# Sixteen blocks of edge rows, and ten tiles of nodes finished beside the last expert

## The chip, the cores and the metric

The kernel runs on one core of a Trainium2 chip. The metric is the device time of one execution in microseconds. The core has the engines PE (TensorE, matrix products), DVE (VectorE), ACT (ScalarE), POOL (GpSimd) and SP (SyncE, which here only issues DMAs). POOL issues DMAs too: all gathers and scatters, and some plain ones.

## The reference

A graph network of four layers over 3125 nodes with 256 features and 50000 edges. Each layer is a graph part and an expert part, both added to `x`. The change concerns the expert part of layer 0, and a little of what is checked before the layers begin:

```python
def _L0_ffn_ref(x, W_gat, att_src, att_dst, b_gat, ln_gamma, ln_beta, W1, b1, W2, b2, edge_index):
    ...
    h = (x_flat @ W_gat).reshape(M, HEADS, NUM_EXPERTS)          # 4 heads, 4 experts
    a_src = (h * att_src).sum(-1)
    a_dst = (h * att_dst).sum(-1)
    e = jax.nn.leaky_relu(a_src[src] + a_dst[dst], negative_slope=0.2)
    e_max = jax.ops.segment_max(e, dst, num_segments=M)
    ee = jnp.exp(e - e_max[dst])
    denom = jax.ops.segment_sum(ee, dst, num_segments=M)
    alpha = ee / (denom[dst] + 1e-16)
    msg = h[src] * alpha[:, :, None]
    agg = jax.ops.segment_sum(msg, dst, num_segments=M).reshape(M, HEADS * NUM_EXPERTS) + b_gat
    scores = _layernorm(agg, ln_gamma, ln_beta).reshape(M, HEADS, NUM_EXPERTS).mean(1)
    topk_s, topk_i = jax.lax.top_k(scores, TOP_K)                # the best 2 of 4
    w = jax.nn.softmax(topk_s, axis=-1)
    for ei in range(NUM_EXPERTS):
        g = jnp.where(topk_i == ei, w, 0.0).sum(-1)
        hh = jax.nn.gelu(x @ W1[ei] + b1[ei], approximate=False)
        out = out + g[..., None] * (hh @ W2[ei] + b2[ei])
```

`edge_index` of this part has 32768 edges, beside a loop at each node. After it the layer 1 graph part begins with a normalization of the new `x`, so it needs every expert's part of a node's row.

## The kernel before

**Layout.** Nodes lie in 25 tiles of 128 (`NT`, `P`), one node to a partition; `X` (25 x 256 floats a partition) stays in SBUF through all layers. `CHUNKS` are six groups of four tiles and one of a single tile: the seven chunks of columns that an expert works on.

**Order.** The framework puts the instructions of every engine into one order ahead of time, by dependencies, by the order in which they were written and by its own estimates of cost; each engine then runs its own order, and waits where a datum or a buffer isn't there. `with tc.issue_after(x)` makes the instructions written in it come behind `x` on `x`'s engine. A pool's tile name has as many buffers as the pool says (2 in `gx` and `wp`); a new tile of the name waits until the oldest is no longer read.

**Survey** (L63 to L208). Before the layers, faults in the indices are counted in the columns of `fault`, summed over the partitions by one matmul (L195) and the columns added (L197). `bad` chooses between the ordered arm (`body` with a plan), which is the one that runs here, and a general one. `gcnt` holds for each node the number of its edges; column 3 asks that none has more than `GK` = 40.

**The routed layer** (`routed_layer_in_order`, L1208). The edges have been ordered by destination before: `gsorted` holds the source of each, `gstart_i` the place where a node's edges begin. Then:

- `router_nodes` normalizes `X`, transposes it into `xt` and computes `hg`, `a_src` and `a_dst`. `node` (20 floats a node: `a_src` and `hg`) goes to DRAM as `nodes` (L1223).
- POOL gathers the row of each edge's source: 256 gathers of 128 rows (L1234, issued in the helper `gather`, L237). Edge `p*256+j` is in partition `p`, so the eight writes (L1236), each of 32 gathers, put a part of every partition's range into `edges`, and the table is only in order when all eight are done.
- The four experts run in `routed_experts` (L1194). A chunk is eight matmuls of 512 columns (L1204, `l0f_ph`), four gelus on ACT (L1205), sixteen matmuls of `project` (L580, `l0f_po`) and two evictions on DVE with the bias (L1292, called `put`). The values of expert 0 stay in SBUF (`y_first`), those of the others go to DRAM (`ytab`, L1294, on SP).
- `shares(d0, ...)` (L1250) takes five tiles of nodes. Five gathers fetch 40 consecutive rows of `edges` for each node (L1255), DVE adds `a_dst`, applies the leaky rectifier, masks what is past a node's count (`off`, L1261), subtracts the maximum; ACT takes the exp (L1265); DVE sums it (`den_`), multiplies the values by it (L1268) and adds them up in halves (L1273 to L1275, `num`). It is called behind chunks 2 to 6 of expert 3; its first DVE work stands behind the chunk's last eviction, its exp behind the chunk's last gelu.
- `router_gates` (L1118) makes the gates for all 25 tiles from `num` and `den_`: some forty small DVE instructions with a sqrt and an exp on ACT between them.
- The value steps (L1303 to L1314): `X += y * gate`, one DVE instruction per tile and expert, first for `y_first`, then with `l0f_yr` tiles of four tiles of nodes that SP loads from `ytab`.

Then `typed_values` (L1418) normalizes `X` again (`normalize`, L456: `bn_stats`, a reciprocal root for tiles 0 to 9, 10 to 19, 20 to 24, and one DVE instruction a tile), transposes it (L469) and begins the products of layer 1 (L1462).

Of the kernel before, what the change touches and what calls it, by code (L numbers as in the profile page):

```python
# [16 lines left out]
P = 128  # L17
# [24 lines left out]
GK = 40  # L42

# [19 lines left out]
def survey(ctx, tc, A):  # L63
# [9 lines left out]
    with ExitStack() as st:  # L73
# [70 lines left out]
        fault = sp.tile([P, 5], F32, name="sv_fault")  # L144
        V.memset(fault, 0.0)
        V.tensor_tensor(junk, nxt, ids["dst"], op=OP.is_lt)
# [47 lines left out]
        faults = ps.tile([1, 5], F32, name="sv_faults")  # L194
# [16 lines left out]
def body(ctx, tc, A, out, plan):  # L211
# [906 lines left out]
    def router_gates(ga, gate, sums, ones_):  # L1118

        den = ga.tile([P, NT, 4], F32, name="den")  # L1120
        V.tensor_scalar(den, ones_, 1e-16, None, op0=OP.add)
        V.reciprocal(den, den)
        ag = ga.tile([P, NT, 16], F32, name="ag", tag="hg")
        prod = ga.tile([P, NT, 16], F32, name="ag_sq", tag="prod")
        V.tensor_tensor(
            ag.rearrange("p t (h c) -> p t h c", h=4), sums, den[:, :, :, None].to_broadcast([P, NT, 4, 4]), op=OP.mult
        )
        bg = load(ga, bcast_rows(A["L0_ffn_b_gat"], 16), [P, 16], "bg")
        lg = load(ga, bcast_rows(A["L0_ffn_ln_gamma"], 16), [P, 16], "lg")
        lb = load(ga, bcast_rows(A["L0_ffn_ln_beta"], 16), [P, 16], "lb")  # L1130

        def all_tiles(x):
            return x[:, None, :].to_broadcast([P, NT, 16])

        V.tensor_tensor(ag, ag, all_tiles(bg), op=OP.add)
        mu = ga.tile([P, NT], F32, name="mu")
        V.tensor_reduce(mu, ag, axis=AX.X, op=OP.add)
        V.tensor_scalar(mu, mu, 1.0 / 16, None, op0=OP.mult)
        V.tensor_tensor(ag, ag, mu[:, :, None].to_broadcast([P, NT, 16]), op=OP.subtract)
        V.tensor_tensor(prod, ag, ag, op=OP.mult)  # L1140
        var = ga.tile([P, NT], F32, name="var")
        V.tensor_reduce(var, prod, axis=AX.X, op=OP.add)
        V.tensor_scalar(var, var, 1.0 / 16, None, op0=OP.mult)
        rs = ga.tile([P, NT], F32, name="rs")
        rsqrt(rs, var, EPS, ga, [P, NT])
        V.tensor_tensor(ag, ag, rs[:, :, None].to_broadcast([P, NT, 16]), op=OP.mult)
        V.tensor_tensor(ag, ag, all_tiles(lg), op=OP.mult)
        V.tensor_tensor(ag, ag, all_tiles(lb), op=OP.add)
        sc = ga.tile([P, NT, 4], F32, name="sc")
# [3 lines left out]
        rank = ga.tile([P, NT, 4], F32, name="rank")  # L1153
        beats = ga.tile([P, NT, 4], F32, name="beats")
        for j in range(4):
            to = beats if j else rank
            V.tensor_tensor(to[:, :, : j + 1], sc[:, :, j : j + 1].to_broadcast([P, NT, j + 1]), sc[:, :, : j + 1], op=OP.is_gt)
            if j < 3:
                V.tensor_tensor(to[:, :, j + 1 :], sc[:, :, j : j + 1].to_broadcast([P, NT, 3 - j]), sc[:, :, j + 1 :], op=OP.is_ge)
            if j:  # L1160
                V.tensor_tensor(rank, rank, beats, op=OP.add)
        best = ga.tile([P, NT], F32, name="best")
        V.tensor_reduce(best, sc, axis=AX.X, op=OP.max)
        V.tensor_tensor(sc, sc, best[:, :, None].to_broadcast([P, NT, 4]), op=OP.subtract)
        S.activation(sc, sc, AF.Exp)
# [3 lines left out]
        V.tensor_tensor(gate, gate, best[:, :, None].to_broadcast([P, NT, 4]), op=OP.mult)  # L1169
# [38 lines left out]
    def routed_layer_in_order():  # L1208

        with ExitStack() as st:  # L1210
# [5 lines left out]
            with ExitStack() as st2:  # L1216
# [7 lines left out]
                part = load(ga, gsorted[:, :].rearrange("(p j) o -> p (j o)", p=P), [P, GT], "src_parts", I32)  # L1224
# [4 lines left out]
                by_part = edges[:GE, :].rearrange("(p j) w -> p j w", p=P)  # L1229
                gx = pool(st2, "gat_e", 2)  # L1230
                for j0 in range(0, GT, 32):
                    ge = gx.tile([P, 32, 20], F32, name="ge")
                    for j in range(32):
                        gather(ge[:, j, :], nodes[:, :], part[:, j0 + j : j0 + j + 1])  # L1234

                    G.dma_start(by_part[:, j0 : j0 + 32, :], ge)  # L1236
# [4 lines left out]


                off = ga.tile([P, NT, GK + 1], F32, name="gat_off")
                V.tensor_tensor(
                    off, iota_f[:, None, : GK + 1].to_broadcast([P, NT, GK + 1]), plan["gcnt"][:, :, None].to_broadcast([P, NT, GK + 1]), op=OP.is_ge
                )
                V.tensor_scalar(off, off, NEG, None, op0=OP.mult)
                V.memset(off[:, :, GK:], 0.0)

                def shares(d0, dve, act):  # L1250

                    el = gx.tile([P, 5, GK + 1, 20], F32, name="el")
                    ds_ = slice(d0, d0 + 5)
                    for i in range(5):
                        gather(el[:, i, :GK, :].rearrange("p k w -> p (k w)"), edges[:, :], gstart_i[:, d0 + i : d0 + i + 1])  # L1255
                    with tc.issue_after(dve):
                        V.tensor_copy(el[:, :, GK, :], node[:, ds_, :])
                        s = gx.tile([P, 5, GK + 1, 4], F32, name="gat_s")
                        V.tensor_tensor(s, el[:, :, :, :4], a_dst[:, ds_, None, :].to_broadcast([P, 5, GK + 1, 4]), op=OP.add)
                        V.scalar_tensor_tensor(s, s, 0.2, s, op0=OP.mult, op1=OP.max)  # L1260
                        V.tensor_tensor(s, s, off[:, ds_, :, None].to_broadcast([P, 5, GK + 1, 4]), op=OP.add)  # L1261
                        V.tensor_reduce(top, s.rearrange("p d k h -> p d h k"), axis=AX.X, op=OP.max)
                        V.tensor_tensor(s, s, top[:, :, None, :].to_broadcast([P, 5, GK + 1, 4]), op=OP.subtract)
# [1005 lines left out]
```

## Time and profile before

| | us |
|---|---|
| three runs | 4818.13, 4819.55, 4824.78 |
| median | 4819.55 |
| the profiled execution | 4826.61 |
| its span in the profile | 4824.8 |
| busy in the span: PE, DVE, POOL, ACT | 4057.4, 2288.3, 1537.9, 1176.9 |
| the routed layer, from its first statistics (before 780) to layer 1's first transposed tile | to 1328.3 |
| the first matmul of the experts | 825.2 |
| the last matmul of the experts | 1222.1 |
| POOL: first gather of edge rows, last fetch of 40 rows | 835.0, 1234.8 |
| gates' last instruction | 1279.6 |
| value steps | 1279.9 to 1320.3 |
| PE's continuous run in layer 1 begins | 1348.4 |

The profile covers one execution. "Span" is the time from the first to the last instruction in it. In the lists, a line such as `L1234` is a line of the kernel; a line of a helper stands for all its callers, so the tile names tell them apart. "`a <- b`" is what an instruction writes and reads. Behind "idle before" stands what ended the idle time of the engine.

### The profile page before, as it was taken

What the parts mean: (1) busy time and instruction counts of PE and PEld (TensorE: products, weight loads), DVE (VectorE), ACT (ScalarE), POOL (GpSimd) and SP (SyncE); (2) the same over time, 40 slices, a digit from 0 to 9 for tenths busy, and PEclk for the clock granted to TensorE, in tenths of its full rate; (3) what the DMA queues carried; (4) which work ended last, traced back from release to release, by engine and by line L of the source; (5) the groups of instructions that cost most, each with busy time, mean ns of one, the idle gap of its engine ahead of it and who ended that gap; (6) DMA issues with size and microseconds to landing.
All of it is one profiled execution on the core that took longest, in us unless ns stands there. A gap on an engine that the chain in (4) does not pass through costs nothing. (4 is left out here: it accounts for less than half of the span.)

```text
span 4824.8 us, 54503 instructions
## 1 busy us (share of the span) xinstructions
PE 4057.4 (84%) x19973; PEld 2509.5 (52%) x20057; DVE 2288.3 (47%) x6392; ACT 1176.9 (24%) x2842; POOL 1537.9 (32%) x1497
## 2 busy tenths in 40 slices
PE   2488888996199996777699999899999997969989
PEld 2355544664066665555575555544444454634556
DVE  8987443112942237777668998610101033260053
ACT  0267721221122223444413222310202011210022
POOL 2067640775000007777505777300000002200010
PEclk6588889998599997887799999999999998989989
DMA  1046582122523347777524432022222322334200
GB/s 57 13 162 196 193 269 66 40 67 80 174 96 134 123 153 210 206 207 206 172 71 142 147 128 82 3 82 89 65 84 67 99 93 74 105 131 153 101 23 28
DMA packets 286835, 553.41 MB, mean 115 GB/s; under 512 B 81979, under 2 KB 195149, under 8 KB 275677
## 3 DMA queue, kind: packets, MB, share of 16 engines
q1 hardware_dynamic: 215804, 411.42, 25.4%
q0 software_dynamic: 70752, 138.40, 10.9%
q8 instruction: 160, 2.62, 0.2%
q14 instruction: 119, 0.97, 0.1%
HBM read 377.47 MB, written 172.20 MB: 114 GB/s over the span
## 5 line engine op out<-in xcount | busy, mean ns | idle before, releaser
L562 PE MATMUL agg_ps<-tt,h_l 128*128 128x512 bf16 (+3 forms) x3796 | 882.5, 394 | 56.8 <-ACT h_l L2049 46.3
L237 POOL DMA_INDIRECT h_kv<-kv_tab,kv_row x416 | 421.9, 1014 | 189.4 <-issue 68.2
L562 PEld LDWEIGHTS <-h_l 128*128 128x128 bf16 x3150 | 290.5, 98 | 331.7 <-issue 16.2
L240 POOL DMA_INDIRECT wgt_cells<-cw_wsum,cw_to x391 | 392.9, 1005 | 168.4 <-issue 112.2
L240 POOL DMA_INDIRECT gsorted<-gs_i,gpos x256 | 313.1, 1223 | 262.5 <-DVE gpos L913 176.7
L1646 PE MATMUL h_pq<-h_q,h_odt 128*128 128x256 bf16 x1248 | 219.6, 340 | 152.4 <-DVE h_qk L1648 152.3
L237 POOL DMA_INDIRECT ge<-nodes,src_parts x256 | 241.8, 945 | 232.9 <-PE l0f_po L580 155.2
L1846 DVE TENSOR_TENSOR at<-agg_ps,rdeg_r 128x512 f32<-128x512 f32 (+1 forms) x42 | 25.6, 633 | 586.5 <-PE agg_ps L562 586.5
L1966 POOL IOTA trash_slot<- 128x32 f32 x1 | 0.2, 158 | 863.4 <-PE l2g_ph L1865 863.4
L1791 ACT ACTIVATE l1f_h<-l1f_ph,bn_shift,bn_scale 128x512 f32<-128x512 f32 (+1 forms) x224 | 162.7, 731 | 384.9 <-PE l1f_ph L1788 384.9
L1646 PEld LDWEIGHTS <-h_odt 128*128 128x128 bf16 x1248 | 142.8, 118 | 209.7 <-issue 159.6
L562 PEld LDWEIGHTS agg_ps<-tt,h_l 128*128 128x128 f32 x700 | 126.3, 192 | 191.6 <-issue 190.9
L580 PE MATMUL l0f_po<-l0f_w,l0f_ht 128*128 128x256 f32 x800 | 180.6, 383 | 45.3 <-ACT l0f_ht L1205 45.3
L580 PE MATMUL l1f_po<-l1f_Wo,l1f_h 128*128 128x256 f32 x800 | 204.3, 388 | 2.3 <-DVE X L1797 1.4
L1697 PE MATMUL h_po<-h_kv,h_of 128*128 128x256 f32 x832 | 194.5, 394 | 8.1 <-DVE h_kv L1693 4.6
L1866 ACT ACTIVATE ht_next<-l2g_ph,l_bhid 128x512 f32<-128x512 f32 (+1 forms) x42 | 26.9, 641 | 714.4 <-PE l2g_ph L1865 714.4
L1788 PE MATMUL l1f_ph<-l1f_h,l1f_W 128*128 128x512 f32 (+1 forms) x448 | 195.4, 559 | 1.1 <-ACT l1f_h L1791 0.6
L580 PEld LDWEIGHTS l0f_po<-l0f_w,l0f_ht 128*128 128x128 f32 x800 | 153.4, 193 | 77.2 <-ACT l0f_ht L1205 46.1
L1788 PE MATMUL l1f_ph<-xt,l1f_W 128*128 128x512 f32 (+1 forms) x448 | 191.3, 547 | 0.9 <-PE l1f_pl L597 0.9
L580 PEld LDWEIGHTS l1f_po<-l1f_Wo,l1f_h 128*128 128x128 f32 x800 | 146.4, 190 | 84.0 <-issue 27.9
L469 PE MATMUL pt<-ident,xn 128*128 128x128 f32 x300 | 63.7, 369 | 149.6 <-DVE xn L458 109.9
L1204 PE MATMUL l0f_ph<-xt,l0f_w 128*128 128x512 f32 (+1 forms) x448 | 178.9, 549 | 3.0 <-ACT l0f_ht L1205 2.1
(628 smaller groups left out, 7482.7 us busy)
## 6 DMA issues: line engine op xcount, KB each, us to landing
tt<-cnt_ds SPq DMA_DIRECT2D x90, 640.0 KB
kv_tab<-kv SPq DMA_DIRECT2D x50, 1024.0 KB
tt<-wgt_cells SPq DMA_DIRECT2D x30, 1280.0 KB
wgt_cells<-cw_zero SPq DMA_DIRECT2D x6, 5800.0 KB
cw_row<-cell_r SPq DMA_DIRECT2D x23, 1128.0 KB
cw_ew<-in_ew_r_dram SPq DMA_DIRECT2D x22, 1108.0 KB
cnt_ds<-row_ds SPq DMA_DIRECT2D x150, 128.0 KB
cnt_sd<-cols SPq DMA_DIRECT2D x6, 3200.0 KB
```

Of the source, the lines that this page charges most:

```text
L237: return G.indirect_dma_start(out=dst, out_offset=None, in_=table, in_offset=bass.IndirectOffsetOnAxis(ap=idx, axis=0))
L240: G.indirect_dma_start(out=table, out_offset=bass.IndirectOffsetOnAxis(ap=idx, axis=0), in_=src, in_offset=None, **kw)
L469: T.transpose(pt[:, j, :], src[:, g + j, h * P : (h + 1) * P], ident)
L562: T.matmul(acc[h][:, :width], part[:, s, h * P : (h + 1) * P], tt[:, s - s0, :width], start=(s == 0 and i == 0), stop=(s == NT - 1 and i = ...
L580: T.matmul(psum, lhs[:, i, t * P : (t + 1) * P], rhs[:, i, :], start=(i == 0), stop=(bias is None and i == k - 1))
L1204: T.matmul(ph[:, :cl], w1[:, k, f * P : (f + 1) * P], xt[:, k, c : c + cl], start=(k == 0), stop=(k == 1))
L1646: T.matmul(pq[:, j, :], w["odt"][:, k0 + j, :], w["q3"][:, part, :], start=(part == 0), stop=(part == 2))
L1697: T.matmul(po, of[:, j, :], kv[:, j, D:], start=(k0 + j == 0), stop=(k0 + j == K - 1))
L1788: T.matmul(ph[:, :cl], ws[layer][:, k, o * P : (o + 1) * P], src[:, k, at : at + cl], start=(k == 0), stop=(k == 1))
L1791: S.activation(dst[:, o, :cl], ph[:, :cl], AF.Relu, bias=shi[:, col], scale=sca[:, col])
L1846: V.tensor_tensor(at[:, hf, c : c + cl], psum, rdeg_r[:, c : c + cl], op=OP.mult)
L1866: S.activation(nt_[:, o, c : c + cl], ph[:, :cl], AF.Relu, bias=b_hid[:, o : o + 1])
```

## The change

- `gsorted` is cut into sixteen blocks of 2048 consecutive edges instead of eight parts that run through all partitions, so the first blocks hold the edges of the first nodes. The tiles are divided into six parts, `GPARTS`: first tile, number of tiles, and the number of blocks that must be written before their fetches. Parts of 5 and 5 tiles need 6 and 11 blocks, 3 tiles need 14, and three of 4 tiles need all.
- The generator `rows_of_edges` writes the blocks that a part needs, gathers one block ahead, fetches the part's rows and yields. Two parts are asked for before the experts, and one more after each `shares`. Since a fetch of 40 rows can reach beyond what is written, the table is first filled with zeros (`blank`), and the survey counts as a fault any of the first three parts whose edges end later than its blocks allow.
- `off` now holds `a_dst` and the mask together, so one addition in `shares` goes.
- `shares` of part 0 stands behind chunk 1 of expert 2, part 1 behind chunk 2 of expert 3, the other four behind the last chunk. `gates` for tiles 0 to 9 stand at chunk 3 of expert 3, the exp in them behind its last gelu.
- All four experts' values go to `ytab`. For tiles 0 to 9 they are loaded on SP into `y_early` and added to `X` behind chunk 4 (experts 0 and 1) and chunk 5 (experts 2 and 3) of the last expert. The other fifteen tiles are loaded on POOL's queue after the gates.

The diff, shortened; `router_gates` has the same instructions on `n` instead of `NT` tiles, its three rows are loaded by `router_rows`, and its exp is put behind `ready` where that is given:

```diff
+GB = 16
+GPARTS = [(0, 5, 6), (5, 5, 11), (10, 3, 14), (13, 4, GB), (17, 4, GB), (21, 4, GB)]
+GEARLY = 10
...
-        fault = sp.tile([P, 5], F32, name="sv_fault")
+        fault = sp.tile([P, 8], F32, name="sv_fault")
         V.memset(fault, 0.0)
+        ready = sp.tile([1, 3], F32, name="sv_ready")
+        for i, (_, _, b) in enumerate(GPARTS[:3]):
+            V.memset(ready[:, i : i + 1], float(b * GE // GB - GK))
...
+        total_g = ps.tile([1, NT], F32, name="sv_total_g")
+        T.matmul(total_g, ones[:, :1], gcnt, start=True, stop=True)
+        upto_g = sp.tile([1, 3], F32, name="sv_upto_g")
+        for i, (d0, n, _) in enumerate(GPARTS[:3]):
+            V.tensor_reduce(upto_g[:, i : i + 1], total_g[:, : d0 + n], axis=AX.X, op=OP.add)
+        V.tensor_tensor(fault[:1, 5:8], upto_g, ready, op=OP.is_gt)
...
+                per = GT // GB
+                part = ga.tile([P, GB, per], I32, name="src_parts")
+                nc.sync.dma_start(part, gsorted[:, :].rearrange("(b p j) o -> p b (j o)", p=P, b=GB))
...
+                by_block = edges[:GE, :].rearrange("(b p j) w -> b p j w", p=P, b=GB)
                 gx = pool(st2, "gat_e", 2)
...
+                def rows_of(b):
+                    if b not in ge:
+                        ge[b] = gx.tile([P, per, 20], F32, name="ge")
+                        for j in range(per):
+                            gather(ge[b][:, j, :], nodes[:, :], part[:, b, j : j + 1])
+
+                def rows_of_edges():
+
+                    done = 0
+                    for d0, n, upto_block in GPARTS:
+                        for b in range(done, upto_block):
+                            rows_of(b)
+
+                            G.dma_start(by_block[b], ge[b])
+                        done = upto_block
+
+                        if done < GB:
+                            rows_of(done)
+                        el = gx.tile([P, 5, GK + 1, 20], F32, name="el")
+                        for d in range(n):
+                            gather(el[:, d, :GK, :].rearrange("p k w -> p (k w)"), edges[:, :], gstart_i[:, d0 + d : d0 + d + 1])
+                        fetched.append(el)
+                        yield
+
+                blank = gx.tile([P, 5, GK + 1, 20], F32, name="el").rearrange("p d k w -> p (d k w)")[:, :1280]
+                V.memset(blank, 0.0)
+                nc.sync.dma_start(edges[:GE, :].rearrange("(p a b) w -> p a (b w)", p=P, a=4), blank[:, None, :].to_broadcast([P, 4, 1280]))
...
+                off = ga.tile([P, NT, GK + 1, 4], F32, name="gat_off")
+                V.tensor_scalar(past, past, NEG, None, op0=OP.mult)
+                V.tensor_tensor(
+                    off, past[:, :, :, None].to_broadcast([P, NT, GK + 1, 4]), a_dst[:, :, None, :].to_broadcast([P, NT, GK + 1, 4]), op=OP.add
+                )
+
+                rows = rows_of_edges()
+                next(rows)
+                next(rows)
...
-                        V.tensor_tensor(s, el[:, :, :, :4], a_dst[:, ds_, None, :].to_broadcast([P, 5, GK + 1, 4]), op=OP.add)
+                        V.tensor_tensor(s, el[:, :, :, :4], off[:, ds_], op=OP.add)
                         V.scalar_tensor_tensor(s, s, 0.2, s, op0=OP.mult, op1=OP.max)
-                        V.tensor_tensor(s, s, off[:, ds_, :, None].to_broadcast([P, 5, GK + 1, 4]), op=OP.add)
...
+                def take(y, e, t0, end, dve=None):
+
+                    n = min(4, end - t0)
+                    (nc.sync if dve is not None else G).dma_start(y[:, :n], ytab[e][:, t0 : t0 + n, :])
+                    for t in range(t0, t0 + n):
+                        with tc.issue_after(dve) if dve is not None else ExitStack():
+                            V.scalar_tensor_tensor(X[:, t, :], y[:, t - t0, :], gate[:, t, e : e + 1], X[:, t, :], op0=OP.mult, op1=OP.add)
...
-                    ys = y_first[:, t0 : t0 + n, :] if e == 0 else wp.tile([P, 4, D], F32, name="l0f_ys")[:, :n]
+                    ys = wp.tile([P, 4, D], F32, name="l0f_ys")[:, :n]
...
-                    if e:
-                        nc.sync.dma_start(ytab[e][:, t0 : t0 + n, :], ys)
-
-                    k = c // 512 - 2
-                    if e == 3 and k >= 0:
-                        shares(5 * k, put.ins, last.ins)
...
+                    nc.sync.dma_start(ytab[e][:, t0 : t0 + n, :], ys)
+
+                    for i, at in enumerate([(2, 1), (3, 2), (3, 6), (3, 6), (3, 6), (3, 6)]):
+                        if at == (e, c // 512):
+                            shares(i, put.ins, last.ins)
+                            next(rows, None)
+                    if (e, c // 512) == (3, 3):
+                        gates(0, GEARLY, last.ins)
+                    if e == 3 and c // 512 in (4, 5):
+                        for t0 in range(0, GEARLY, 4):
+                            for i in range(2):
+                                take(y_early[:, GEARLY * i :][:, t0:GEARLY], 2 * (c // 512 - 4) + i, t0, GEARLY, put.ins)
+
+                y_early = stage[0].tile([P, NT, D], F32, name="l0f_y_early", tag="xn")
                 routed_experts(wp, ps, b1, xt, keep)
-                router_gates(ga, gate, num.rearrange("p t (h c) -> p t h c", h=4), den_)
+                gates(GEARLY, NT)
             with ExitStack() as st2:
                 yp = pool(st2, "l0f_yp", 3)
...
+                for t0 in range(GEARLY, NT, 4):
+                    for e in range(4):
+                        take(yp.tile([P, 4, D], F32, name=f"l0f_yr{e}"), e, t0, NT)
```

## The prediction

> **What bounds the kernel now.** I read the page first, then the waits and busy times between 780 and 1420 us, then the timelines of the engines there.
>
> ```profile
> span 4824.8 us, 54503 instructions
> ...
> PE   2488888996199996777699999899999997969989
> DVE  8987443112942237777668998610101033260053
> ...
> POOL 2067640775000007777505777300000002200010
> ```
>
> A slice is 120.6 us. PE is full nearly everywhere, with a hole in the eleventh slice (1206 to 1327 us), where DVE shows 9 and then 4: the end of the routed layer.
>
> ```profile
> 825.00:1137.00 312.00, 311.21 (x1110) 207.46 (x1110) 33.35 (x53) 66.64 (x101) 229.47 (x246) 1.00 0.22 50
> 1137.00:1183.00 46.00, 0.73 (x2) 0.50 (x2) 8.17 (x7) 2.86 (x3) 26.51 (x29) 0.53 0.33 100
> 1183.00:1222.00 39.00, 37.25 (x138) 26.22 (x136) 35.81 (x33) 13.66 (x18) 10.73 (x10) 0.94 0.40 132
> 1222.00:1328.00 106.00, 0.13 (x1) 0.00 (x0) 98.10 (x221) 7.63 (x9) 4.73 (x5) 0.52 0.52 174
> ```
>
> Columns: stretch, length, busy PE, PEld, DVE, ACT, POOL, granted clock, DMA share, GB/s. The experts run at full rate to 1137, stand for 46 us, end at 1222, and then PE waits 106 us for DVE. The waits say who ends each hole:
>
> ```profile
> PE pt L469 <- DVE xn L458: 107.1, 2, 106.2
> ...
> DVE gat_s L1259 <- DMA el<-edges,gstart_i: 45.9, 1, 45.9
> ACT gat_s L1265 <- DVE gat_s L1263: 65.5, 4, 45.5
> ...
> PE l0f_po L580 <- ACT l0f_ht L1205: 45.3, 1, 45.3
> ```
>
> The first hole is a queue: the first shares' exp stands in ACT's order before a gelu, the exp waits for DVE, and DVE for edge rows that POOL fetches.
>
> ```profile
> 1160.64 0.58 POOL L1236 DMA_DIRECT2D edges<-ge  x1 [1.99 <-DMA ge<-nodes,src_parts]
> 1163.39 0.97 POOL L237 DMA_INDIRECT el<-edges,gstart_i  x1 [2.17 <-DMA edges<-ge]
> ...
> 1261.36 0.33 SPq L1415 DMA_DIRECT2D ty_r<-in_type_r_dram  x1
> ...
> 1279.93 29.29 SPq L1311 DMA_DIRECT2D l0f_yr<-l0f_y  x21
> ```
>
> POOL starts at 835.0 and has all 256 gathers and eight writes out only at 1160.64. Later, loads of expert values start at 1279.93, when the gates are done.
>
> From 1350 to 1700 us every 50 us hold 50.00 us of PE work at clock 1.00, so what PE gains before 1350 is kept behind it, one for one. My mark is 1348.4, where PE becomes continuous (L1462).
>
> **The change part by part.** *Survey.* One matmul, three reduces, one compare. Rows of the same size: L195 0.19 us, L197 0.15 us, with gaps 0.2 to 0.3, so 0.2 + 0.3 + 4 x 0.17 = 1.2 us. The body's first instructions start at 66.1, where a DMA issued at 62.50 has just landed, while the fault flag is done at 63.12; that may hide all. Bounds 0 and +1.5; I take +1.2.
>
> *Start of the layer.* The index load now comes in 64-byte runs; it is issued at 785.7 and used at 835.0, so 49 us cover it. A memset of 1280 elements (L1442, 1024 in 0.91: 1.1 us) and a write of 2.6 MB of zeros are added. At the 289 GB/s of 1262 to 1280 the write takes 9 us. SP has nothing between 803.4 and 827.5, and the first block is written only at 855. Should it meet the node table (issued 827.5), POOL starts up to 9 us later: 0 to +9, I take 0. The 4100-element add that makes the offsets (L1268: 3280 in 3.56, so 4.45 us) fits before DVE's first eviction at 836.5 (8.57 us idle). In return 1.03 us (L1261) leaves each shares call.
>
> *POOL's order.* Gathers follow each other every 1.249 us, and a write adds 0.6 (878.75 to 880.60 holds one gather and one write). First rows: 112 gathers and 6 writes, then five fetches. They start at 835.0 + 112 x 1.249 + 6 x 0.6 = 978.5. Five fetches took from 1163.39 to 1173.74, 10.4 us, to land, so they are there at 989. The shares that use them stand behind the eviction of expert 2, chunk 1: 1026.7 + 0.7. Second: 197 gathers before, 11 writes, so start 1087.7 and landing at 1098, against an eviction at 1126.9. So both exps find their data, with 38 and 29 us to spare, and the 45.3 us stall goes. A write after fetches must wait until they have landed, because they read the same table: with two block buffers at most one further block (20 us) can be put ahead of a fetch, which stays inside that room.
> Fourth part: 269 gathers, 16 writes, then the last block must land and be written and land: 2.0 + 2.2 as at 1158 to 1163. 835.0 + 336.0 + 9.6 + 4.2 = 1184.8. The three waits for fetches to land cost 0 (other gathers fill them) to 4.4 each (1169.3 to 1173.7); I take 3 in all: 1188. Landing of four fetches, 9 us: 1197 (bounds 1194 and 1207).
>
> *The last expert.* An expert takes 86.5 us (last evictions 912.64 and 999.13), so without stalls the last eviction is at 1172.1. Added to ACT: two exps with sqrt and exp of the early gates, each with table loads of 1.28 on both sides. In 1183 to 1222 three such breaks cost PE 39.0 - 37.25 = 1.75 us; at worst each costs 1.28 + 0.89 + 1.28 = 3.45. Four breaks: 2 to 14 us, I take 5, so PE ends at about 1177.
> The Trainium skill, page "ScalarE: Activation LUTs", section "What ACT_TABLE_LOAD costs", has 2.66 us for every switch, of which 1.38 is a drain. The row disagrees: the load at 1204.36 lasts 1.28 and its gelu starts at 1205.65. By the rule the four breaks would be at most 4 x 6.2 = 25 us, by the row at most 14.
> DVE from 1127 on: shares 14.5 (the sum of the rows of L1257 to L1275 without L1261), gates 10 (before 18.7, less four memsets of 0.91, a wait of 2.6 and 2.5 for the smaller tiles), forty value steps at 0.40 = 16, seven evictions 4.4: 45 us in the 50 until 1177. It just fits; the early loads, twelve more on SP, where only seven stores an expert stand, have 14 us between chunks. In 1183 to 1222 DVE was 92% busy and PE still ran at 95%.
>
> *Shares of the last fifteen tiles.* Three tiles: 9.5 us, from 1177, done by 1190, before the fourth part's rows land. Then three times four tiles, 12 each (14.5 x 0.8 = 11.6 if proportional, 14.5 at most): 1197 + 36 + 1 for an exp = 1234. The fetches of parts five and six need buffers that come free at 1190 and 1209, and land 9 us after, before their turn.
>
> *Gates and values.* Before, 1261.2 to 1279.9, 18.7 us, of which four memsets are 3.6 and a wait for `pri` 2.6. The later layer's loads that hold `pri` back start when the shares' buffers are free, as at 1261.36. With fifteen tiles instead of 25: 12 to 18.7, I take 16. The first value step then needs loads: expert 0's values no longer lie in SBUF, which covered that time with 9.98 us of L1306. A POOL write took 2.75 from issue to landing (1160.64 to 1163.39): +3. First step at 1253. Sixty steps at 28.98/73 = 0.397: 23.8, to 1277.
> The sixteen loads move from SP to POOL. Before, 9.4 MB came in 29.29 us; now 7.5 MB need 23.4 us at that rate, as much as DVE needs.
> The Trainium skill, "SBUF — State Buffer", section "Who interferes with whom", speaks against this: a DVE instruction with two SBUF inputs blocks a GpSimd instruction that reads SBUF. By it each of the sixteen issues could wait a whole step, 16 x 0.48 = 8 us if nothing hid it. Beside a busy DVE 25 fetches took 0.997 on average instead of 0.945, 16 x 0.05 = 1 us, so I add nothing.
>
> *Behind the values.* From the last step (1320.3) to PE's continuous run (1348.4) are 28.1 us of DVE statistics and normalization. Ten tiles are now finished early. Their statistics (10 x 0.56) and normalization (3.3) may fill DVE's waits. Bounds 0 and -13 (with a share of the transposes' copies); I take -6.
>
> **The sum.** 1277 + 28.1 - 6 = 1299 against 1348.4: -49.4; with the survey +1.2: -48. The profiled execution took 4826.6 us (1.8 outside its span), 7.1 over the median of the three runs shown, 4819.55; the difference is set against that median: 4772 us. The likeliest case's own range is 4752 to 4790.
>
> **Rivals.** *Early values slip.* DVE has 45 us of work in a room of 50. If gates and value steps of the ten tiles end up behind the last expert, 26 us return to DVE's tail: 4772 + 26 = 4798. For it: DVE takes instructions in order, and a wait for sqrt or a load holds all behind it. Against: the 92% above.
> *The order itself is the new wait.* Shares of part four placed ahead of part three's second half leave DVE standing until 1197 with 8 us undone, and a late POOL start adds 9: 4789. For it: at 1191.84 the next group's L1259 ran between an earlier group's L1273s.
> *POOL's queue bounds the tail (slower).* If loads issued on POOL land one after another at L1236's rate, 320 KB in 2.75, then 7.5 MB take 66 us instead of 23.8, +42. The next layer's loads (5.6 MB on SP, 19 us) share the same stretch: 4772 + 42 + 19 = 4833. It decides above 4.5 us a load ((23.8 + 48)/16). For it: no row shows large loads on that queue. Against: 2.75 is mostly time to land, and gathers issued every 1.25 overlap.
> *The change does not do what it says*: the first exp still waits. That needs rows 38 us later than reckoned; the stall would be back and only the ten tiles' move would remain, about 4819 - 15 = 4804.
>
> **How the numbers follow.** Forecast 0.60; early values slip 0.13; the order 0.09; no early exp 0.04; POOL's queue 0.08; what I have not seen 0.06, half of it slower. About 0.2%, 9.6 us, is what a measurement can tell from no change. Forecast, slip and order are faster, and most of the fourth: 0.83 with a little of the rest; same 0.06; slower 0.11. The range 4745 to 4805 takes in the bounds above (landing 1194 to 1207, breaks 2 to 14, normalization 0 to -13) and the two mild rivals.
>
> **What would show it.** Right: no PE wait above 10 us between 825 and 1170; the last eviction between 1172 and 1186; the fourth part's rows landed by 1207; sixty value steps within 30 us; PE continuous near 1300. Wrong: an exp that waits over 10 us for DVE in the experts; forty value steps behind the last expert; gaps between the last sixty steps that end on a DMA.

## The result, and the profile after

The changed kernel takes 4805.85 us (median of 8 runs, 4803.55 to 4810.51), the kernel before 4823.22 us beside it (8 runs, 4818.13 to 4824.78): ratio 0.9967, 95% interval 0.9958 to 0.9976. That is 17 us faster, where 48 were forecast, and 0.85 us above the upper end of the range. The profiled execution has a span of 4801.7 us against 4824.8.

From the page of the changed kernel: span, and busy tenths in 40 slices (120.0 us each).

```profile
span 4801.7 us, 54722 instructions
...
PE   2488888997099987677699999899999997969978
...
DVE  8987443124732337777669998600101033260053
...
POOL 2067640777100017777406777300000002200010
```

PE's hole is still in the eleventh slice (1200 to 1320 us), now with a 0 in it. The same stretches as before, with the same columns (stretch, length, busy PE, PEld, DVE, ACT, POOL, granted clock, DMA share, GB/s):

```profile
1137.00:1183.00 46.00, 38.05 (x148) 26.33 (x147) 36.37 (x93) 15.06 (x22) 37.47 (x30) 0.96 0.35 104
1183.00:1222.00 39.00, 0.00 (x0) 0.00 (x0) 8.14 (x14) 1.29 (x2) 16.12 (x18) 0.50 0.28 85
1222.00:1328.00 106.00, 13.77 (x63) 10.03 (x64) 95.16 (x239) 12.02 (x18) 16.14 (x24) 0.52 0.48 159
```

The first hole is gone: the experts run on and end at 1175.6 us. But from 1183 to 1222 us DVE, which has to do the rest, works 8.14 of 39 us. The waits between 780 and 1420 us (engine, tile, line, what it waited for: us in total, times, longest) and POOL's timeline (start, us, operation, idle time before and its end) name the reason.

```profile
POOL l0f_yr L1339 <- DVE gate L1189: 37.1, 1, 37.1
DVE gat_s L1314 <- DMA el<-edges,gstart_i: 32.9, 2, 20.4
...
POOL el L250 <- DVE el L1312: 23.5, 1, 23.5
```

```profile
1037.31 3.91 POOL L250 DMA_INDIRECT ge<-nodes,src_parts  x1 [0.30 <-issue]
...
1138.57 3.27 POOL L250 DMA_INDIRECT ge<-nodes,src_parts  x1 [0.30 <-issue]
...
1161.53 5.24 POOL L250 DMA_INDIRECT ge<-nodes,src_parts  x1 [0.30 <-issue]
...
1177.55 3.66 POOL L250 DMA_INDIRECT ge<-nodes,src_parts  x1 [0.30 <-issue]
...
1193.99 0.94 POOL L250 DMA_INDIRECT el<-edges,gstart_i  x1 [0.30 <-issue]
...
1201.85 1.15 POOL L1270 DMA_DIRECT2D edges<-ge  x2 [4.42 <-DMA el<-edges,gstart_i]
1205.39 1.00 POOL L250 DMA_INDIRECT el<-edges,gstart_i  x1 [2.39 <-DMA edges<-ge]
...
1233.74 0.95 POOL L250 DMA_INDIRECT el<-edges,gstart_i  x1 [23.54 <-DVE el L1312]
```

Four single gathers took 3.9, 3.3, 5.2 and 3.7 us; eight more take 1.1 to 1.6, the others 0.94. Then come the third part's fetches (1193.99), behind all of block 15's gathers; then both remaining writes, which waited 4.42 us until those fetches had landed; then the fourth part's fetches (1205.39); and the fifth part's only at 1233.74, after 23.54 us of waiting for a buffer. DVE's timeline shows what it did with the rows:

```profile
1201.34 0.67 DVE L1314 TENSOR_TENSOR gat_s<-el,gat_off 128x492 f32<-128x492 f32 x1 [20.39 <-DMA el<-edges,gstart_i]
1214.53 0.84 DVE L1314 TENSOR_TENSOR gat_s<-el,gat_off 128x656 f32<-128x656 f32 x1 [12.52 <-DMA el<-edges,gstart_i]
...
1232.89 0.58 DVE L1329 TENSOR_REDUCE gat_num<-el 128x48 f32<-128x240 f32 x1
```

The first line is the third part (3 tiles, 492 = 3 x 41 x 4), the second the fourth. In DVE's order the fourth part's add stands directly behind the third's, so the third part, whose rows were there at 1201, is summed only at 1232.89. The shares end at 1269.8, the gates at 1280.0, the value steps run from 1284.93 to 1309.1, and PE's first typed product follows at 1319.65. The first product with `lin_v` starts at 1333.44, before at 1353.59: 20.15 us earlier.

### The profile page after: what moved, and what is told of

It is laid out like the page before. It is cut to its first block, busy times and chain, and to the rows that moved or that the text cites. A ratio compares the mean times of both kernels' runs of the same rounds, so it can differ in the third digit from the quotient of the medians.

```text
span 4801.7 us, 54722 instructions
## 1 busy us (share of the span) xinstructions
PE 4045.5 (84%) x20059; PEld 2493.3 (52%) x20059; DVE 2295.5 (48%) x6445; ACT 1182.8 (25%) x2849; POOL 1568.8 (33%) x1521
## 5 line engine op out<-in xcount | busy, mean ns | idle before, releaser
L1712 PE MATMUL h_pq<-h_q,h_odt 128*128 128x256 bf16 x1248 | 205.9, 324 | 161.8 <-DVE h_qk L1714 161.6
L250 POOL DMA_INDIRECT ge<-nodes,src_parts x256 | 257.2, 1005 | 232.9 <-PE l0f_po L593 155.2
L1763 PEld LDWEIGHTS h_po<-h_kv,h_of 128*128 128x128 f32 x832 | 160.4, 195 | 31.7 <-DVE h_kv L1759 5.4
L1714 DVE TENSOR_TENSOR h_qk<-h_kv,h_pq 128x512 f32<-128x512 f32 (+1 forms) x220 | 141.6, 650 | 60.9 <-DMA h_kv<-kv_tab,kv_row 48.5
## 6 DMA issues: line engine op xcount, KB each, us to landing
tt<-wgt_cells SPq DMA_DIRECT2D x30, 1280.0 KB
```

The source lines that it names most:

```text
L250: return G.indirect_dma_start(out=dst, out_offset=None, in_=table, in_offset=bass.IndirectOffsetOnAxis(ap=idx, axis=0))
L1712: T.matmul(pq[:, j, :], w["odt"][:, k0 + j, :], w["q3"][:, part, :], start=(part == 0), stop=(part == 2))
L1714: V.tensor_tensor(qk[:, :n], kv[:, :n, :D], pq[:, :n], op=OP.mult)
L1763: T.matmul(po, of[:, j, :], kv[:, j, D:], start=(k0 + j == 0), stop=(k0 + j == K - 1))
```

## Experiments

All edits are against the changed kernel, and L numbers are its lines. Ratios are to the kernel before, run beside each set. "Shares' end" is the end of the last L1329 in the profile (in `no_edges`, whose lines are shifted, L1332). Each profile is one execution. Where the kernel before takes 4822 us, the first gather of edge rows starts between 833.9 and 836.9 us, at 836.85 in the changed kernel's profile: up to 3 us between two profiles can be this start and not the edit.

**The first set** asked which of three things in series held the tail: POOL's order, DVE's order, the buffers. Its kernels ran where the kernel before takes 5699 us, with PE and ACT standing up to 100 us at a time beside POOL's gathers, so that the experts end at 1648 to 1662 us, long after POOL: its ratios say little of the 17 us and are not to be held against 0.9967.

`pool_order`: a block's gathers wait, on POOL, for the last fetch ahead of them.

```diff
-                        for j in range(per):
-                            gather(ge[b][:, j, :], nodes[:, :], part[:, b, j : j + 1])
+                        with tc.issue_after(fetch[-1]) if fetch else ExitStack():
+                            [gather(ge[b][:, j, :], nodes[:, :], part[:, b, j : j + 1]) for j in range(per)]
...
+                            at = gather(el[:, d, :GK, :].rearrange("p k w -> p (k w)"), edges[:, :], gstart_i[:, d0 + d : d0 + d + 1])
+                        fetched.append(el), fetch.append(at.ins)
```

> POOL's order alone is put right: the gathers of a block wait, on POOL, for the last fetch that stands ahead of them in the program, so the three fetches of the third part go ahead of the last twelve gathers of block 15. My theory is that three things in series cost the tail: POOL's order, DVE's order and the two fetch buffers. By it the third part's rows land at 1179 instead of 1201 us, but DVE still has the fourth part's add ahead of the rest of the third part, so that gives nothing by itself; the writes no longer wait 4.4 us for the fetches: the fourth part lands at 1211 instead of 1214.5 and the stage ends 3 to 4 us earlier (time -0.1%). The rival, that POOL's order alone is what was lost, has the shares' end 15 to 20 us earlier (-0.4%).

`dve_order`: from the fourth part on, a part's first two steps stand behind the last reduce of the part before.

```diff
-                    with tc.issue_after(dve):
+                    with tc.issue_after(summed[-1] if i > 2 else dve):
...
-                    V.tensor_reduce(num[:, ds_, :], el[:, :, :5, 4:].rearrange("p d k w -> p d w k"), axis=AX.X, op=OP.add)
+                    summed.append(V.tensor_reduce(num[:, ds_, :], el[:, :, :5, 4:].rearrange("p d k w -> p d w k"), axis=AX.X, op=OP.add).ins)
```

> DVE's order alone: the copy and the add that begin the shares of parts four, five and six stand behind the last reduce of the part before. My theory: the third part is then done at 1210 us, in time in which DVE stood idle; its buffer comes free 23 us earlier, so the fifth part's rows are there when the fourth is done (1226.5), and the shares end at 1250 instead of 1269.8: time -20 us (-0.4%). The rival, that POOL's order alone is what was lost, has under 5 us here. A second rival, stretched gathers, has nothing here.

`both_orders` has both edits.

> Both orders. My theory: third part done by 1195 us, fourth from 1211 to 1223, the shares end at 1245 to 1247 instead of 1269.8, time -23 us (-0.5%), so the two are not a sum of equals: DVE's order is most of it. The rival (POOL's order alone) has here what it has without DVE's order, -15 to -20.

`third_buffer`: the fifth part's rows go into the tile of the early values (tag `xn`).

```diff
-                        el = gx.tile([P, 5, GK + 1, 20], F32, name="el")
+                        el = gx.tile([P, 5, GK + 1, 20], F32, name="el") if d0 != 17 else stage[0].tile([P, NT, D], F32, name="el_x", tag="xn").rearrange("p t d -> p (t d)")[:, :4100].rearrange("p (d k w) -> p d k w", d=5, k=GK + 1)
```

> A third buffer for fetched rows: the fifth part's rows go into the tile that held the early values, so that their fetches need not wait for the fourth part. My theory, buffers as the smallest of the three terms: POOL's idle 23.5 us before the fifth part's fetches goes, its shares start 8 us earlier, the sixth part's fetches still wait for a buffer; shares' end 6 us earlier (-0.12%). If the buffers were the main cause: shares' end 15 us or more earlier.

Measured: 0.9957 (0.9941 to 0.9973), 0.9998 (0.9979 to 1.0017), 0.9956 (0.9939 to 0.9973), 0.9971 (0.9953 to 0.9988). The ratios alone would speak for the rival that POOL's order was what was lost, but the traces don't: the copy L1312 of the third part, which stands behind the last expert, starts at 1653.0, 1667.2, 1656.3 and 1664.7 us, and the differences between the ratios follow it in the main. The two kernels with POOL's order have their experts done some 10 us earlier; why was not tried. What can be read is the tail behind that copy, to the shares' end: 56.1, 55.2, 55.3 and 46.6 us. With the third and fourth parts' rows landed long before, DVE's order is worth 1 us and the buffer 9, both against `pool_order`; the changed kernel itself is not in this set.

**Orders, one more time, with two new questions.** The two orders were run again, where the kernel before takes 4822 us; all sets from here on ran so.

> DVE's order alone, once more: in the first set every kernel, the one before too, took 18% longer than in its own profile (5699 us against 4823), with PE, ACT and DVE standing still for up to 100 us at a time while POOL gathered, so the experts ended long after POOL and the orders hardly met. Where the kernel before takes 4823 us, my theory has the third part done at 1210 us, the shares' end at 1250 instead of 1269.8 and a ratio to the kernel before of 0.9925 (the changed kernel has 0.9967). The rival, POOL's order alone: 0.996 to 0.997. Where the kernel before takes 5700 us again: 0.998 to 1.000, as in the first set.

Measured: 0.9934 (0.9920 to 0.9947). DVE's timeline:

```profile
1200.07 0.67 DVE L1314 TENSOR_TENSOR gat_s<-el,gat_off 128x492 f32<-128x492 f32 x1 [21.46 <-DMA el<-edges,gstart_i]
...
1211.94 0.59 DVE L1329 TENSOR_REDUCE gat_num<-el 128x48 f32<-128x240 f32 x1
...
1213.75 0.84 DVE L1314 TENSOR_TENSOR gat_s<-el,gat_off 128x656 f32<-128x656 f32 x1 [0.98 <-DVE rs_r L448]
...
1255.25 0.73 DVE L1329 TENSOR_REDUCE gat_num<-el 128x64 f32<-128x320 f32 x1
```

The adds of the third and the fourth part start about 1 us earlier than before the edit (1200.07, 1213.75), but the third part is now summed at 1211.94 instead of 1232.89, in time that DVE had stood idle. The shares end at 1256.0, 13.8 us earlier (14 of the 20 expected), and PE's first typed product comes at 1305.76, 13.9 earlier. Of the 13.8, 0.8 are the rows and 13 the edit: from the fourth part's add to the shares' end are 42.2 us where the changed kernel has 55.3.

> Both orders once more. Where the kernel before takes 4823 us: my theory has the fourth part from 1211 to 1223, the shares' end at 1245 to 1247 and a ratio of 0.992; the rival (POOL's order is what was lost, DVE's nothing) has the same with and without DVE's order and a ratio of 0.993 to 0.994. Where it takes 5700 us: 0.9956, as in the first set.

Measured: 0.9940 (0.9926 to 0.9954), shares' end 1256.5. The third part's fetches go out at 1169.70 and it is summed at 1192, 20 us earlier than with DVE's order alone, and nothing comes of it: the fourth part's fetches still start at 1204.97. POOL has the same gathers to make before them in whichever order. So DVE's order is the loss, and POOL's adds nothing to it that can be seen: counted from the first gather (835.45 here, 833.93 in `dve_order_2`) the shares end 1 us earlier. POOL's order alone was run only in the first set.

`one_input`: the forty early value steps read X alone; the experts' values of ten tiles are left out.

```diff
-                            V.scalar_tensor_tensor(X[:, t, :], y[:, t - t0, :], gate[:, t, e : e + 1], X[:, t, :], op0=OP.mult, op1=OP.add)
+                            if dve is not None:
+                                V.tensor_scalar(X[:, t, :], X[:, t, :], gate[:, t, e : e + 1], 0.0, op0=OP.mult, op1=OP.add)
+                            else:
+                                V.scalar_tensor_tensor(X[:, t, :], y[:, t - t0, :], gate[:, t, e : e + 1], X[:, t, :], op0=OP.mult, op1=OP.add)
```

> The forty early value steps read X alone (X times gate plus zero) and leave the experts' values of ten tiles out; their loads and their place stay. It asks what stretched single gathers to 3.3, 5.2 and 3.7 us. If DVE instructions with two inputs from SBUF keep POOL from its descriptors: the gathers beside the early steps go back to 0.94 us, only the one beside the shares' product (3.3 us) stays, and the rows of blocks 14 and 15 are there some 9 us earlier; the time falls by 5 to 9 us from the changed kernel's 0.9967 to 0.995 to 0.996. If DMA traffic or a busy DVE of any kind stretched them: the same long gathers, and a time within 2 us of the changed kernel's.

Measured: 0.9942 (0.9929 to 0.9956), shares' end 1260.2, 9.6 us earlier; 2.1 of them are the earlier start of this execution (first gather at 834.72). The early steps and the first fetch of the third part, from the timelines of DVE and POOL:

```profile
1156.32 6.11 DVE L1343 TENSOR_SCALAR X<-X,gate 128x256 f32<-128x256 f32 x20
...
1170.76 6.39 DVE L1343 TENSOR_SCALAR X<-X,gate 128x256 f32<-128x256 f32 x20
```

```profile
1184.58 0.95 POOL L250 DMA_INDIRECT el<-edges,gstart_i  x1 [0.30 <-issue]
```

DVE is busy in two runs of over 6 us, and no gather beside them takes over 1.1 us; the fetches start 9.4 us earlier than at 1193.99. The 3.3 us gather beside the shares' product L1322 stays, as expected. One doubt was left: with y unread, its loads come earlier too, so traffic could be the cause.

`no_survey` leaves the survey's new limits out.

```diff
-        for i, (_, _, b) in enumerate(GPARTS[:3]):
-            V.memset(ready[:, i : i + 1], float(b * GE // GB - GK))
...
-        T.matmul(total_g, ones[:, :1], gcnt, start=True, stop=True)
...
-        V.tensor_tensor(fault[:1, 5:8], upto_g, ready, op=OP.is_gt)
```

> The survey's three new limits and the product that they need are left out; all else stays. My prediction had +1.2 us for them, the trace shows the layer starting 2.0 us later (836.9 against 835.0). If the survey is the cause of that start: the first gather at 834.9 to 835.1 and a ratio 0.0004 under the changed kernel's 0.9967. If the start moved for another reason: no change in the first gather's start.

Measured: 0.9960 (0.9947 to 0.9974), which can't be told from 0.9967; the first gather starts at 836.15, not at 835. The expectation fails: eight profiles in which the survey has its limits and the kernel before takes 4822 us start that gather between 833.9 and 836.9. So the 2 us between the one profile of before and the one of after can't be put down to the survey.

**The third set** settled the stretched gathers and asked what they and the tail are worth. `two_x` is `one_input` with two inputs again, X both times; the same values are left out.

```diff
-                                V.tensor_scalar(X[:, t, :], X[:, t, :], gate[:, t, e : e + 1], 0.0, op0=OP.mult, op1=OP.add)
+                                V.scalar_tensor_tensor(X[:, t, :], X[:, t, :], gate[:, t, e : e + 1], X[:, t, :], op0=OP.mult, op1=OP.add)
```

> As the one-input kernel, but the forty early steps take X twice (X times gate plus X, two SBUF inputs); again the experts' values of ten tiles are left out of the sum, and their loads hold nothing up. It differs from the one-input kernel in the number of inputs alone, with the loads at the same place. If two inputs are what keeps POOL's gathers: one gather beside each run of twenty steps ends about 0.8 us after the run's last step (5.2 and 3.7 to 4.8 us long), the third part's rows start at 1192 to 1194 and the ratio is the changed kernel's, 0.9967 (0.996 to 0.9975). If the loads' traffic stretched them: 0.94 us each and the one-input kernel's 0.9942.

Measured: 0.9962 (0.9949 to 0.9976). DVE's runs and the long gathers beside them:

```profile
1157.39 8.00 DVE L1343 SCALAR_TENSOR_TENSOR X<-X,gate 128x256 f32<-128x256 f32 x20
1171.83 8.00 DVE L1343 SCALAR_TENSOR_TENSOR X<-X,gate 128x256 f32<-128x256 f32 x20
```

```profile
1162.55 3.66 POOL L250 DMA_INDIRECT ge<-nodes,src_parts  x1 [0.30 <-issue]
...
1175.80 4.84 POOL L250 DMA_INDIRECT ge<-nodes,src_parts  x1 [0.30 <-issue]
```

The runs end at 1165.39 and 1179.83, the gathers at 1166.21 and 1180.64: 0.82 and 0.81 us behind. So the loads' traffic is not the cause. Counted from the first gather of each, the third part's fetches start at 357.5 us here and at 349.9 in `one_input`: 7.6 us is the price. The operation changes with the number of inputs (`tensor_scalar` to `scalar_tensor_tensor`), but the shares' product L1322, a `tensor_tensor` with two inputs, holds a gather too, and the reduce L1320 with one input (1135.91 + 1.63 in the changed kernel) has gathers of 0.94 us beside it. So the second input does it.

`dve_one` joins `dve_order` and `one_input`.

> DVE's order and one-input early steps together (the values of ten tiles are left out). Alone they moved the shares' end from 1269.8 to 1256.0 and to 1260.2 us. If the two losses stand in series they add: shares' end at 1246 to 1247, ratio 0.991. If one hides the other: 1255 or later and 0.993.

Measured: 0.9917 (0.9904 to 0.9931), shares' end 1247.6: 22.2 of the 23.4 us that the two have alone (2 to 3 us of either sum are the start, 836.85 against 834.40 here). The losses stand in series.

`late`: `dve_order`, with all early steps behind the last eviction.

```diff
-                    if e == 3 and c // 512 in (4, 5):
-                        for t0 in range(0, GEARLY, 4):
-                            for i in range(2):
-                                take(y_early[:, GEARLY * i :][:, t0:GEARLY], 2 * (c // 512 - 4) + i, t0, GEARLY, put.ins)
...
+                    for pair in range(2 if (e, c // 512) == (3, 6) else 0):
+                        for tt in range(0, GEARLY, 4):
+                            for i in range(2):
+                                take(y_early[:, GEARLY * i :][:, tt:GEARLY], 2 * pair + i, tt, GEARLY, put.ins)
```

> DVE's order, and all forty early steps behind the last eviction, in the stretch in which DVE stands idle until the third part's rows land (1178 to 1200 us), instead of in two runs beside the last expert. If a run of two-input steps keeps a gather to its end: only the run after 1178 costs POOL, some 4 us instead of 9.6, the fourth part's rows land at 1207 to 1209 instead of 1213.7, shares' end 1250 to 1252 instead of 1256, ratio 0.9922 to 0.993. If the steps delay the third part by more than that: 1256 or later.

Measured: 0.9938 (0.9924 to 0.9951), shares' end 1257.2: a miss. The evictions, no longer behind value steps, end earlier, so the steps start at 1174.62 and not at 1178, and they run without a break:

```profile
1174.62 15.91 DVE L1342 SCALAR_TENSOR_TENSOR X<-l0f_y_early,gate,X 128x256 f32<-128x256 f32 x40
```

```profile
1180.56 10.78 POOL L250 DMA_INDIRECT ge<-nodes,src_parts  x1 [0.30 <-issue]
```

One gather of 10.78 us, to 1191.34, is about as dear as the two of 5.23 and 4.84 us in `dve_order_2`. Beside POOL's gathers the steps cost about the same in both places.

`no_edges`: `dve_order`, with tiles 17 to 24 taken from the node table; the survey gains a column.

```diff
+        V.tensor_reduce(fault[:, 8:9], gcnt[:, 17:], axis=AX.X, op=OP.max)
...
-GPARTS = [(0, 5, 6), (5, 5, 11), (10, 3, 14), (13, 4, GB), (17, 4, GB), (21, 4, GB)]
+GPARTS = [(0, 5, 6), (5, 5, 11), (10, 3, 14), (13, 4, GB)]
...
+                V.tensor_copy(num[:, 17:, :], node[:, 17:, 4:])
+                V.memset(den_[:, 17:, :], 1.0)
```

> DVE's order, and the last two parts (tiles 17 to 24) are not fetched: the survey takes the general path instead if one of their nodes has a routed edge, and without edges the share of the node's own row is 1, so their sums are copies of the node table. It asks what stands behind the last landing. If the tail is bound by DVE's shares, 13 us a part: the shares end at 1229 to 1231 instead of 1256 and the ratio falls by 0.0054 to 0.988. If it is bound by POOL's or DMA's work, or what was idle takes up the ten tiles' statistics, which lay between the parts: a gain under 15 us, 0.990 to 0.993.

Measured: 4763.22 us (4 runs, 4758.33 to 4766.09) against 4821.32, ratio 0.9881 (0.9866 to 0.9896), the fastest of all here. Shares' end 1229.9 and PE's first typed product at 1280.05, both 26 us before those of `dve_order_2`: behind the last landing the tail is DVE's, 13 us a part. `no_edges` serves graphs whose routed edges all end in the first 2176 nodes, as here; any other takes the general path.

## Why the prediction was wrong, step by step

**Right.** *The start*: the write of zeros delays nothing. *No stall in the experts*: exps at 1034.38 and 1134.99 find their rows, the first fetches start at 980.47 (978.5 reckoned) and 1094.81 (1087.7). *The last expert*: PE ends at 1175.6 (1177 reckoned), the early gates take 10 us and all forty early steps fit, so "early values slip" did not come. *The sixty last steps*: 24.2 us (23.8). *POOL's queue*, the slower rival: the loads are issued 0.53 us apart and hold up no step but the first, as the changed kernel's timelines of POOL and DVE show.

```profile
1280.58 4.27 POOL L1339 DMA_DIRECT2D l0f_yr<-l0f_y  x8 [37.11 <-DVE gate L1189]
```

```profile
1284.93 6.42 DVE L1342 SCALAR_TENSOR_TENSOR X<-l0f_yr,gate,X 128x256 f32<-128x256 f32 x16 [4.97 <-DMA l0f_yr<-l0f_y]
```

Eight loads go out in 4.27 us; the first step waits 4.97 us (3 reckoned), and sixteen steps run without a gap. Of the marks named beforehand, three held: PE's longest wait among the experts is 0.7 us, the last eviction stands at 1180.30, the sixty steps are done within 30 us. Two did not: the fourth part's rows (1214.53 for 1207) and PE (1319.65 for about 1300). None of the three signs of being wrong showed.

**The step that failed** is "Shares of the last fifteen tiles", with "Fourth part" under it: "Three tiles: 9.5 us, from 1177, done by 1190", rows of the fourth part at 1197, shares' end at 1234. It was 1269.8, 36 us later. The parts of that:
- *The order itself is the new wait*, 13 us, shown by `dve_order_2`. It was my rival at 0.09, with 8 us for this wait, and it was the case. I had taken the parts to run one behind the other, as the program has them; in the trace of before a group's L1259 ran between an earlier group's steps, which I quoted for the rival and did not believe. While the fourth part's add waited 12.52 us, the third part was not summed. The third part's buffer was not free either, and the fifth part's fetches stood 23.54 us; that cost nothing further, for from 1214.53 on DVE never waits for rows.
- *Gathers stretched by two-input instructions*, about 15 us of the 17.5 by which the fourth part's add comes late (1214.53 for 1197). Beside the early steps the gathers take 7.8 us more than at 0.94 each, and `one_input` against `two_x` shows that the second input is the cause (7.6). Beside the products and sums of the first two parts (L1322, L1327) they take 7.2 us more: 3.91, 1.55 and 1.20 us from 1037.31, and 3.27, 1.55, 1.20 and 1.10 from 1138.57. These 7.2 are read from the trace alone; no run leaves them out. I had added up POOL's gathers at 1.249 us apiece, which has 0.94 for the gather itself.
- *The rest of the 17.5*: the first gather starts at 836.85 for 835.0, 1.9 us; POOL's waits for landings were 1.24, 4.42 and 2.39, 8.1 in all where I took 4.2 + 3 = 7.2, so these were right within 1 us.
- *The size of the shares*, 5 us: with DVE's order put right, 42.2 us from the fourth part's add to the end against 37. The fourth part takes 16, with the normalization of ten tiles between its steps, the others 13 each where I took 12.
- The survey's +1.2 could not be seen.

The block order of POOL, which I had not foreseen either (block 15's gathers ahead of the third part's fetches), cost at most 1 us by `both_orders_2`.

**Sizes.** Gates took 10.1 us for 16 reckoned (-6): the next layer's loads, with the memsets behind them, now start at 1309.23, behind the value steps instead of among the gates. The first step's wait adds 2. Behind the values, from the last step to the first product with `lin_v`, 24.3 us instead of 33.3: -9 where I took -6. So -49.4 + 36 - 6 + 2 + 0.4 - 3 = -20, which is the 20.15 us measured at `lin_v`. The mark that I had chosen, where PE becomes continuous, moved by 28.8 (1348.40 to 1319.65): it was a poor one, because PE's continuous run now takes in the transposes of fifteen tiles and first products with `lin_k`, part of which lay ahead of the mark before. That the gates and what stands behind the values came out 9 us better than reckoned was luck; without it the change would have won about half as much. The runs show -17 (interval -12 to -20).

**The rule on two inputs.** "Who interferes with whom" in the Trainium skill's "SBUF — State Buffer" says that a DVE instruction with two SBUF inputs contends with a GpSimd instruction that reads SBUF. This case agrees: gathers that read their indices from SBUF are held at two inputs (3.66 and 4.84 us) and not at one. I had weighed the rule at the sixteen loads, where nothing showed (0.53 to 0.54 us each beside the steps), and let a mean of 0.997 us decide. It bit where I had not looked: beside the first two parts' products, and beside forty steps in two unbroken runs. The trace of before had it already, in single rows that the mean hid:

```profile
1194.62 1.01 DVE L1261 TENSOR_TENSOR gat_s<-gat_s,gat_off 128x820 f32<-128x820 f32 x1
```

```profile
1194.98 1.47 POOL L237 DMA_INDIRECT el<-edges,gstart_i  x1 [19.39 <-DVE gat_num L1275]
```

The fetch took 1.47 us instead of 0.94 and ended at 1196.45, 0.82 us behind the two-input L1261.

## What to carry to other kernels

A part that is ready early gains nothing if a part that is ready late stands ahead of it in an engine's order: read the order between two parts from the trace, and pin it where it matters. When work is moved beside another engine that sets the end, price what it does to that engine's instructions, and look at the longest of them, not the mean. Where what is left behind the last landing is all one engine's work, take work out of it; putting it in order won 13 us here, doing without part of it another 26.

## What was not expected of the hardware

A gather held by DVE ends a fixed time behind DVE's run. From DVE's timeline of the changed kernel:

```profile
1036.84 3.56 DVE L1322 TENSOR_TENSOR el<-el,gat_s 128x3280 f32<-128x3280 f32 x1
...
1137.46 3.56 DVE L1322 TENSOR_TENSOR el<-el,gat_s 128x3280 f32<-128x3280 f32 x1
...
1157.95 8.00 DVE L1342 SCALAR_TENSOR_TENSOR X<-l0f_y_early,gate,X 128x256 f32<-128x256 f32 x20
...
1172.39 8.00 DVE L1342 SCALAR_TENSOR_TENSOR X<-l0f_y_early,gate,X 128x256 f32<-128x256 f32 x20
```

The four long gathers end at 1041.22, 1141.84, 1166.77 and 1181.21, each 0.82 us behind the end of its line here; in `two_x` it is 0.82 and 0.81, in `late` 0.81. A gather is held by the run of steps as a whole, not once for each instruction in it; a gap of 0.04 us ends a run (L1327 follows L1322 at 1040.44, and the gather still ends at 1041.22). At the start of a run of 0.4 us steps some gathers still pass (1.2 and 1.3 us in `two_x`) before one is held.

In the first set, engines other than POOL stood still beside its gathers with nothing in the profile that they waited for. From the timeline of `dve_order`, a gelu of the experts:

```profile
1354.05 0.69 ACT L1225 ACTIVATE l0f_ht<-l0f_ph,l0f_b 128x512 f32<-128x512 f32 x1 [100.20 <-issue]
```

From 1000 to 1300 us PE was busy 73 of 300 us there; once POOL's gathers had ended, 100 of 100. What held the engines was not tried. The first set ran on another chip than the later ones.
